# Products along the columns: read u in rows of eight, write the bank with a stride

## The chip, the cores and the metric

The kernel runs on one core of a Trainium2 chip. The core has a matrix engine (TensorE, PE in the profile, with its weight loads as PEld), a vector engine (VectorE, DVE), a scalar engine (ScalarE, ACT), GpSimd (POOL), and SyncE (SP), which issues the transfers here. Matmul results go to PSUM, which this kernel uses as eight banks of 512 fp32 values on each of 128 partitions; everything else on the chip lies in SBUF. The metric is the device time of one execution in microseconds. Before the change the median of three runs is 6957.4 us (6956.57 to 6957.86).

## The reference

Four layers are applied one after the other to an image batch x of shape (4, 192, 56, 56), all in fp32. The first three (a window attention with a convolution, a channel gate, an overlapping window attention with a gated feed-forward part) aren't touched. The last one is a selective scan in four directions, cut here to what matters:

```python
xn = _ln_cf(x, ln_w, ln_b)                                  # norm over the channels
xc, z = split(einsum('dc,bchw->bdhw', in_proj_w, xn))
xc = silu(depthwise_conv3x3(xc) + conv_b)                   # called u in the kernel
x_hw = xc.reshape(Bsz, D, L)                                # pixels by rows
x_wh = xc.transpose(0, 1, 3, 2).reshape(Bsz, D, L)          # pixels by columns
xs = stack([x_hw, x_wh, x_hw[..., ::-1], x_wh[..., ::-1]], axis=1)
x_dbl = einsum('kcd,bkdl->bkcl', x_proj_w, xs)              # 20 numbers a pixel and direction
dts, Bv, Cv = split(x_dbl, [R, R + N], axis=2)              # R = 12, N = 4
dt = softplus(einsum('kdr,bkrl->bkdl', dt_proj_w, dts) + dt_proj_b)
ys = _selective_scan(xs, dt, -exp(A_log), Bv, Cv) + Ds * xs # h = exp(dt A) h + dt B u ; y = C h
y = sum of the four directions, each put back in pixel order
out = x + einsum('cd,bdhw->bchw', out_proj_w, _ln_cf(y) * silu(z))
```

So x_proj (40 outputs for a pair of opposite directions, 192 inputs) is applied to u once in the order of rows and once in the order of columns.

## The kernel before

A layer is one function; the last is `layer3`. The 192 channels lie as two halves of 96 on the partitions (padded with zeros to 128), the 3136 pixels of an image along the free dimension. An image is cut into 7 chunks of 448 pixels: eight rows of 56, or, for the column directions, eight columns of 56.

For each of the four images b and each chunk c, `begin(b, c)` loads x, normalizes it (`layer_norm`, lines 1768 to 1789), projects it (line 1821), convolves with nine matmuls by diagonal matrices for each half (line 1851), applies SiLU and leaves u in one of two SBUF tiles `us[b % 2]`, pixels by rows. It ends with `product(b, 0, ...)` (called on line 1878): x_proj for the two row directions. `begin_columns(b, c)` waits until all seven chunks of an image are there, takes the eight columns of its chunk as a view of u and calls `product(b, 1, ...)` on line 1884.

`product` makes two matmul calls, one for each half of the channels, that accumulate into one bank (line 1893); an fp32 matmul call is two recorded instructions, so a product is four. ACT copies the 40 x 448 result to one of two `prod` tiles (line 1896), and SP writes it to a DRAM buffer `prods[b][o]` (line 1899), whose pixels are in the order of rows (o = 0) or of columns (o = 1).

A step of the scan is a chunk in one direction. `load` fetches the 12 rows for dt (line 1964) and, spread over partitions, B and C (line 1970); `sizes` makes dt (matmul 1985, softplus 1997); `decay` spreads dt over four states by transfers (line 2023) and exponentiates (2031); `scan` forms dt u on DVE (line 2046 by rows, 2049 with a column view of u), spreads it with PE (2056), multiplies by B (2062), scans on DVE (2078), multiplies by C on POOL (2085), sums over states with PE (2101) and adds to y (2106, 2111 or 2115; the last reads the bank with a stride to put columns back). Directions run in the order rows, columns, columns backward, rows backward. `final(b, c)` normalizes y, multiplies by the gate (line 1920, POOL), projects (1929), adds x (1940) and writes out.

The order of the work is set before anything runs, by a planner in the program, the class `Order`. Every piece of work is a generator that yields, ahead of each step, the engine, a planned duration and the tiles that it takes:

```python
def on_pe(n, *takes, ready=None):
    return "PE", 0.0019 * n, takes, None, ready
...
best.append((t + self.HURRY * th[0], th[1], t, th))   # earliest planned start, plus 0.05 us a place
```

The planner starts the piece with the smallest planned start plus a small term for its place, moves the clock of its engine on by the planned duration, and goes on. The instructions of PE, ACT, DVE and POOL, and with them the transfers on SP, are issued in that order, and each engine works its queue off in order. `product` plans `passes * n` columns of PE time: 2 passes for rows and 4 for columns, where n is 448. A change of a planned duration can thus change the order of everything behind it. The places are set at the end of `layer3`:

```python
order.add(n * (b - 1) + 6 * c + 4, begin(b, c))
order.add(n * (b - 1) + 48 + c, begin_columns(b, c))
order.add(n * (b + 1) - 2 * c, final(b, c))
```

Of the kernel before, what the change touches and what calls it, by code (L numbers as in the profile page):

```python
# [19 lines left out]
B, C, H, W = 4, 192, 56, 56  # L20
HW = H * W
HALF = 96
CH = 448
# [191 lines left out]
def load_packs(nc, pool, packs, aps):  # L215
    tiles = {}
    for name, pack in packs.items():
        t = pool.tile([pack.p, pack.n], F32, name=f"w_{name}")
        nc.sync.dma_start(t, aps[name])
        for n in pack.at:  # L220
            tiles[name + "." + n] = pack.view(t, n)
    return tiles
# [18 lines left out]
class Order:  # L241
# [20 lines left out]
    def take(self, kind="bank"):  # L262
        slot = min((s for s in self.kinds[kind] if s[0] is not None), key=lambda s: s[0])
        slot[0] = None
        return slot[1]

    def done(self, tile):

        (slot,) = (s for slots in self.kinds.values() for s in slots if s[1] is tile)
        slot[0] = self.end + self.LATENCY  # L270
# [53 lines left out]
def on_pe(n, *takes, ready=None):  # L324

    return "PE", 0.0019 * n, takes, None, ready
# [10 lines left out]
def on_act(*n, takes=(), table=None, ready=None):  # L337
    return "ACT", sum(0.2 + 0.0009 * i for i in n), takes, table, ready
# [6 lines left out]
def on_sp(*takes):  # L345
    return "SP", 0.5, takes, None, None
# [1329 lines left out]
def layer3(tc, src, packs, aps, dst):  # L1676
# [7 lines left out]
    nc = tc.nc  # L1684
    with ExitStack() as ctx:
        const = ctx.enter_context(tc.tile_pool(name="c_const", bufs=1))
        dram = ctx.enter_context(tc.tile_pool(name="c_dram", bufs=1, space=DRAM))
        w = load_packs(nc, const, packs, aps)
        inT = w["c128.inT"]
        in_b = const.tile([HALF, 4], F32, name="in_b")  # L1690
        with tc.tile_pool(name="c_ps0", bufs=1, space=PSUM) as ps0:
            pb = ps0.tile([HALF, 4], F32, name="pb")
            for m in range(4):
                for k in range(2):
# [4 lines left out]
                        start=(k == 0),  # L1699
                        stop=(k == 1),  # L1700
# [26 lines left out]
        def keep(name, shape, n, rows=128, zero=True):  # L1727

            tiles = [per.tile([rows, *shape], F32, name=f"{name}{i}") for i in range(n)]
            if zero:  # L1730
                for t in tiles:
                    nc.gpsimd.memset(t[HALF:], 0.0)
            return tiles

        us = keep("u", [2, HW], 2)
# [24 lines left out]
        def gone(*what):  # L1760
            return what in passed
# [30 lines left out]
        def begin(b, c):  # L1792
# [83 lines left out]
            nc.sync.dma_start(pixels(zmem[b])[:, :, c * CH : (c + 1) * CH], zt)  # L1876
            done(zt)
            yield from product(b, 0, px, u[:, :, px], 2)
            passed.add(("rows", b, c))

        def begin_columns(b, c):
            yield lambda: all(gone("rows", b, i) for i in range(NCHUNK))
            uv = us[b % 2].rearrange("p h (y x) -> p h x y", x=W)[:, :, 8 * c : 8 * c + 8]
            yield from product(b, 1, slice(c * CH, (c + 1) * CH), uv, 4)
            passed.add(("columns", b, c))

        def product(b, o, px, u, passes):

            n = px.stop - px.start
            yield on_pe(passes * n, "bank")  # L1890
            pp = take()
            for k in range(2):
                nc.tensor.matmul(pp[:40, :n], w["c128.xpT"][:, k, o], u[:, k], start=(k == 0), stop=(k == 1))  # L1893
            yield on_act(n, takes=("prod",))
            t = take("prod")
            nc.scalar.copy(t[:, :n], pp[:40, :n])
            done(pp)
            yield on_sp()
            nc.sync.dma_start(prods[b][o][:, px], t[:, :n])
            done(t)  # L1900
# [224 lines left out]
        n = 8 * NSC  # L2125
        for b in range(B):
            for c in range(NCHUNK):
# [3 lines that stand above are left out]
# [42 lines left out]
```

## Time and profile before

| | |
|---|---|
| median of three runs | 6957.4 us |
| the profiled execution | 6951.71 us |
| its span, first to last instruction | 6949.9 us |
| mean granted TensorE clock | 0.931 |
| PE busy | 5890.7 us (85%) |
| DVE busy | 5908.5 us (85%) |
| ACT, POOL busy | 2640.6 us (38%), 1423.8 us (20%) |
| line 1893, all products | 224 instructions, 149.5 us of PE |
| rows of that line | 128x448, x192; 128x504, x16; 128x392, x16 |

Times of single instructions come from one profiled execution. A row of a timeline is the start in us, the length, engine, line, operation, output<-inputs and the number of instructions; in brackets stands the idle time of the engine before it, and what ended it. A row of a table of stages is the stretch in us, its length, and for each engine the time in which it was busy, then the share of its full clock that TensorE was granted, the mean share of time that the transfer engines were busy, and the GB/s they moved. Groups and sources are named by the line of the kernel.

### The profile page before, as it was taken

The page shows a single profiled execution, that of the slowest core. Times are in us where ns is not written, and L with a number is a line of the kernel's source. Part 1 is how long each engine was busy: PE and PEld are TensorE (multiplying, and loading weights), DVE is VectorE, ACT ScalarE, POOL GpSimd, SP SyncE. Part 2 cuts the span into 40 slices and gives each one's busy share as a digit, 9 for nine tenths or more (in the row PEclk, how much of TensorE's full clock was granted, in tenths as well). Part 3 has the DMA queues.
Part 4 walks back from the last instruction along what each step waited for, and adds up shares of the span by engine and source line. Part 5 has one row for each costly group of instructions (what it writes and reads, how often), then busy time and mean ns, then how long its engine had stood idle before and what let it go on. Part 6 is the DMA issues. An engine that isn't in the chain of part 4 may idle for free. (4 is left out here: it accounts for less than half of the span.)

```text
span 6949.9 us, 107660 instructions
## 1 busy us (share of the span) xinstructions
PE 5890.7 (85%) x43810; PEld 2685.0 (39%) x43810; DVE 5908.5 (85%) x7379; ACT 2640.6 (38%) x4083; POOL 1423.8 (20%) x1409
## 2 busy tenths in 40 slices
PE   4999979999999994968888787885799989899776
PEld 2445434444444441345444444442332222222211
DVE  2799999999999999648999898997348788887897
ACT  1111112221122211135555455543256656556543
POOL 0000000000000000032222222220125445445564
PEclk9999989999999997979999899987899999999998
DMA  3222112221222112110000000000145555555654
GB/s 94 56 52 64 34 35 53 58 65 35 52 64 61 35 45 73 45 52 16 19 19 14 19 17 17 19 14 8 34 104 130 142 143 129 152 133 136 166 151 108
DMA packets 252044, 462.69 MB, mean 67 GB/s; under 512 B 30388, under 2 KB 237964, under 8 KB 240412
## 3 DMA queue, kind: packets, MB, share of 16 engines
q1 hardware_dynamic: 251548, 455.80, 25.8%
q8 instruction: 345, 5.65, 0.3%
q14 instruction: 151, 1.24, 0.1%
HBM read 238.58 MB, written 62.96 MB: 43 GB/s over the span
## 5 line engine op out<-in xcount | busy, mean ns | idle before, releaser
L789 DVE TENSOR_TENSOR pr<-vdx,attn 112x1792 f32<-112x1792 f32 (+4 forms) x720 | 1185.6, 1648 | 19.0
L634 PE MATMUL a_bank<-qk_in,w_a 64*49 64x392 f32 x9408 | 1156.3, 496 | 0.0
L2085 POOL TENSOR_TENSOR da<-st,bc 128x448 f32<-128x448 f32 x672 | 859.0, 1283 | 862.9 <-DVE st L2078 618.9
L794 DVE TENSOR_TENSOR oa<-oa,pr 112x1792 f32<-112x1792 f32 (+1 forms) x423 | 764.8, 1808 | 0.0
L634 PE MATMUL a_bank<-qk_in,wd 64*49 64x392 f32 x4032 | 689.6, 493 | 0.0
L2078 DVE TENSOR_TENSOR_SCAN st<-da,st,c_bank 128x448 f32<-128x448 f32 x576 | 646.6, 1132 | 0.0
masks.py:197 POOL MEMSET b_ident<- 128x128 f32 x1 | 0.2, 205 | 2856.0 <-DVE sc L1042 2856.0
L634 PEld LDWEIGHTS a_bank<-qk_in,w_a 64*49 64x49 f32 x9408 | 431.6, 120 | 394.1 <-issue 389.2
L2062 DVE TENSOR_TENSOR c_bank<-c_bank,bc 128x448 f32<-128x448 f32 x672 | 382.5, 618 | 153.1 <-PE c_bank L2056 152.5
L315 ACT ACT_TABLE_LOAD x378 | 485.0, 1283 | 6.6
L2031 ACT ACTIVATE da<-da,a_neg 128x448 f32<-128x448 f32 x672 | 414.1, 658 | 122.5 <-DMA da<-dt 117.9
L1343 DVE SCALAR_TENSOR_TENSOR bg<-bzpad,w_b,bg 128x448 f32<-128x448 f32 (+2 forms) x672 | 423.1, 684 | 0.0
L2101 PE MATMUL c_bank<-da,w_c 128*32 128x448 f32 x1344 | 349.5, 570 | 66.3 <-POOL da L2085 61.4
L1851 PE MATMUL c_bank<-pad,diag 128*96 128x448 f32 (+2 forms) x1008 | 396.8, 543 | 2.4 <-ACT pad L1832 2.3
L794 DVE TENSOR_TENSOR ob<-ob,pr 112x1792 f32<-112x1792 f32 (+3 forms) x282 | 393.0, 1394 | 0.0
L2056 PE MATMUL c_bank<-du,w_c 32*128 32x448 f32 x1344 | 257.8, 624 | 121.6 <-DVE du L2046 80.4
L869 PE MATMUL a_bank<-xc,w_a 128*128 128x448 f32 x672 | 296.8, 571 | 66.0 <-DVE xc L854 66.0
L878 ACT ACTIVATE hm<-a_bank,w_a 128x448 f32<-128x448 f32 x168 | 106.4, 634 | 637.4 <-PE a_bank L869 618.3
L634 PEld LDWEIGHTS a_bank<-qk_in,wd 64*49 64x49 f32 x4032 | 247.4, 119 | 256.5 <-issue 254.6
L1432 PE MATMUL bank<-bxn,w_b 128*128 128x448 f32 (+2 forms) x672 | 288.1, 557 | 24.8 <-DVE bxn L1215 18.6
L884 PE MATMUL a_bank<-hm,w_a 128*96 128x448 f32 x672 | 290.6, 564 | 21.3 <-ACT hm L878 21.3
L655 PE MATMUL a_bank<-qk_sum,w_a 64*49 64x168 f32 (+1 forms) x5376 | 277.7, 337 | 27.1 <-DVE qk_sum L625 25.2
(305 smaller groups left out, 9825.2 us busy)
## 6 DMA issues: line engine op xcount, KB each, us to landing
da<-dt SPq DMA_DIRECT2D x672, 224.0 KB
vdx<-vmem SPq DMA_DIRECT2D x168, 476.0 KB
bc<-prod SPq DMA_DIRECT2D x224, 224.0 KB
row<-x SPq DMA_DIRECT2D x56, 336.0 KB
x<-x SPq DMA_DIRECT2D x4, 2352.0 KB
vmem<-vt SPq DMA_DIRECT2D x56, 168.0 KB
xc<-x SPq DMA_DIRECT2D x56, 168.0 KB
mid<-xc SPq DMA_DIRECT2D x56, 168.0 KB
```

The lines of the kernel that those rows point to most:

```text
L315: self.nc.scalar.preload_act_table_set(table)
L634: nc.tensor.matmul(py[a][outs[g], : 7 * W].rearrange("p (y x) -> p y x", x=W), wt[halves[a], dx], q[halves[a], r, i0 + m : i0 + m + 7, dx ...
L789: nc.vector.tensor_mul(pr, vv, wt)
L794: nc.vector.tensor_add(og, og, before)
L869: nc.tensor.matmul(ph[:, :CH], w["a128.c1T"][:, k, 128 * m : 128 * m + 128], xt[:, k], start=(k == 0), stop=(k == 1),)
L1343: nc.vector.scalar_tensor_tensor(dst, x, wt[:, t : t + 1], dst, ALU.mult, ALU.add)
L1851: nc.tensor.matmul(rows2(pc[:HALF, : n * W]), diag[:, h, t], pad[:, h, at + t // 3 : at + t // 3 + n, t % 3 : t % 3 + W], start=(t == 0), ...
L2031: nc.scalar.activation(da, da, AF.Exp, scale=a_neg[:, k, g : g + 1])
L2062: nc.vector.tensor_mul(tiles[j][:, :SCH], tiles[j][:, :SCH], b_)
L2078: nc.vector.tensor_tensor_scan(sts[j][:, r], da[:, r], tiles[j][:, :SCH][:, r], first, ALU.mult, ALU.add)
L2085: nc.gpsimd.tensor_mul(da, sts[j], c_)
L2101: nc.tensor.matmul(py[32 * j : 32 * j + 32, :SCH], w["c128.sum"], das[j], start=True, stop=True)
```

## The change

The view of u that a column product reads keeps the order of the rows: for each of the 56 rows, the eight neighbouring elements of the chunk's columns. The result of each pixel goes to the same place of the bank as before (columns one after the other), which is now 56 elements away from the result before it. The planned PE time of a column product goes from 4 to 2 passes. The matmul of the row products, the copy, the write to DRAM and all that reads it are as they were.

```diff
         def begin_columns(b, c):
             yield lambda: all(gone("rows", b, i) for i in range(NCHUNK))
-            uv = us[b % 2].rearrange("p h (y x) -> p h x y", x=W)[:, :, 8 * c : 8 * c + 8]
-            yield from product(b, 1, slice(c * CH, (c + 1) * CH), uv, 4)
+            uv = us[b % 2].rearrange("p h (y x) -> p h y x", x=W)[:, :, :, 8 * c : 8 * c + 8]
+            yield from product(b, 1, slice(c * CH, (c + 1) * CH), uv, 2)
             passed.add(("columns", b, c))
...
             yield on_pe(passes * n, "bank")
             pp = take()
+
+            out = pp[:40, :n].rearrange("p (x y) -> p y x", y=H) if o else pp[:40, :n]
             for k in range(2):
-                nc.tensor.matmul(pp[:40, :n], w["c128.xpT"][:, k, o], u[:, k], start=(k == 0), stop=(k == 1))
+                nc.tensor.matmul(out, w["c128.xpT"][:, k, o], u[:, k], start=(k == 0), stop=(k == 1))
```

## The prediction

> **What bounds the kernel now.** I read the table of stages first, then PE's order of work around the changed products, then the rows of the instructions that resemble the new one. The last layer starts its work near 4960 us and ends with the span. Stages around the column products (us, then busy time of PE, PEld, DVE, ACT, POOL, the granted TensorE clock, DMA share, GB/s):
>
> ```profile
> 5129.72:5152.90 23.18, 23.18 (x31) 3.71 (x28) 6.35 (x8) 6.13 (x12) 3.62 (x3) 1.00 0.26 72
> ...
> 5461.00:5466.00 5.00, 5.00 (x10) 0.89 (x10) 5.00 (x8) 4.80 (x7) 3.39 (x4) 0.50 0.47 142
> 5462.00:5517.00 55.00, 53.59 (x149) 11.07 (x146) 44.04 (x60) 32.74 (x51) 26.96 (x22) 0.95 0.59 153
> 5515.00:5935.00 420.00, 369.76 (x1224) 119.18 (x1220) 337.86 (x434) 251.54 (x358) 204.37 (x169) 0.95 0.55 137
> ...
> 6500.00:6700.00 200.00, 141.97 (x468) 33.93 (x469) 193.28 (x253) 104.72 (x154) 120.88 (x93) 0.94 0.62 161
> ```
>
> In the first row PE has no idle time while DVE works 6.35 of 23.18 us: this is the run of all seven column products of image 0. In the third row (column products of image 1) PE is busy 97%, DVE 80%; images 2 and 3 look the same (53.01 and 51.83 us of 55). In the fourth PE has 88%. Only in the last part, with no convolution left, is DVE the bound (97%). So PE time of a column product lies mostly on the path. The timeline says so too:
>
> ```profile
> 5129.72 23.26 PE L1893 MATMUL c_bank<-u,w_c 128*40 128x448 f32 x28
> 5152.91 0.95 PE L2101 MATMUL c_bank<-da,w_c 128*32 128x448 f32 x6
> ...
> 5153.98 0.68 DVE L2106 SCALAR_TENSOR_TENSOR y<-u,d_sum,c_bank 96x448 f32<-96x448 f32 x1 [17.81 <-PE c_bank L2101]
> ...
> 5472.76 3.47 PE L1893 MATMUL c_bank<-u,w_c 128*40 128x448 f32 x4
> 5476.16 1.03 PE L2056 MATMUL c_bank<-du,w_c 32*128 32x448 f32 x6
> ```
>
> DVE stood idle 17.81 us because PE reached the sums of line 2101 only after the 28 column instructions. One product is two calls and four recorded instructions. The chain that ended last gives a column product 3.40 us and a 448-wide row product, which reads u densely, 1.63 us. PE's clock isn't the reason for the double price: the neighbouring line 2101 keeps its 0.95 us, and the first row's clock is 1.00.
>
> **Part one, the read.** The column product reads u with 56 elements (224 bytes) between neighbours: 23.26 us by 28 is 0.83 us an instruction, against 1.63 by 4 = 0.41 for the dense row product. DVE shows the same toll on the same view of u:
>
> ```profile
> L2046 DVE TENSOR_TENSOR du<-dt,u x112: 589/595/2599, 5045.5 to 6905.9; 96x448 f32<-96x448 f32 x112
> ...
> L2049 DVE TENSOR_TENSOR du<-dt,u x112: 946/965/1127, 5224.8 to 6785.9; 96x448 f32<-96x448 f32 x112
> ...
> L2111 DVE TENSOR_TENSOR y<-y,c_bank x56: 585/607/618, 5473.0 to 6926.9; 96x448 f32<-96x448 f32 x56
> ...
> L2115 DVE TENSOR_TENSOR y<-y,c_bank x112: 581/612/622, 5239.0 to 6800.1; 96x448 f32<-96x448 f32 x112
> ```
>
> The three numbers are minimum, median and maximum in ns. Line 2049 (u by columns) takes 965 against 595 for line 2046 (u by rows). The new read has runs of eight elements (32 bytes). Nearest row: line 1581 feeds PE 8x8 windows out of a wider image, 233 ns, and line 1639 feeds it 64 dense elements, 221 ns; 12 ns on 64 elements makes 84 on 448. So the new read costs between 0.41 and 0.41 + 0.08 = 0.49 us an instruction. Those windows aren't aligned and the runs of u are (they start at 224 y + 32 c bytes, all multiples of 32), so I take 0.41.
>
> **Part two, the write.** No matmul of this kernel writes neighbouring results apart, so this cost has to be bounded. Below: nothing. It can't be a gain, since the dense write is the row product's. Above, by the nearest row: line 2115 reads the very same pattern (stride 56 within the bank, runs over eight) in 612 ns, line 2111 dense in 607. A visit to a far place in a bank therefore costs no more than 612/448 = 1.37 ns with all fixed time counted in. One visit per element makes at most 448 x 1.37 = 0.61 us an instruction; if accumulating needs two (fetch and put back), 1.22 us.
>
> The Trainium skill speaks against the change: "PSUM — Partial Sum Buffer", Specifications (TRN2), gives the bank lines of two fp32 values and says that an access pattern that isn't contiguous slows matmuls significantly. With half of each line used, the cost by that rule would double, 0.41 to 0.83 us, exactly what the strided read costs today, and the gain would be nothing. Rows 2111 and 2115 show no such loss, but for reads by another engine at 1.3 ns an element. PE delivers a dense fp32 element each 0.41 us/448 = 0.9 ns, not much faster. I take "no cost" as likeliest because the only row with this pattern in a bank is 5 ns off the dense one, and keep both ends (0.41 and 1.22 us).
>
> **Part three, the plan.** The price that the planner uses goes from 4 to 2 passes: 0.0019 x 4 x 448 = 3.40 us becomes 1.70, the old and the (hoped) new measured price. With it the order on all queues may change: PE; the copy (line 1896) on ACT and the write (1899) on SP behind each product; loads (1964, 1970) and spreads (2023) on SP; products with C (2085) on POOL. Nothing is added or dropped: same four PE instructions, one copy, one transfer. I cost the reshuffle at nothing on average; it repeats image by image (the first column products start at 5468, 5943 and 6413), so what it hits it hits three times.
>
> **Part four, what covers what.** In image 0 SP issues the writes of the products one by one, 13.51 us for five, before the next spreads; they come sooner by as much as PE does. The copies alternate between two tiles, though. At 1.63 us a product a tile must be free again in 3.3 us; copy 0.53, issue 0.28, and a landing like the 3.88 us that the chain gives for a spread would make 4.7, so up to 0.7 us a product could be lost there. PE has other banks, so most of that is hidden: 0.8 us lost in all.
>
> **Sum.** Image 0: 23.19 - 7 x 1.63 = 11.8 us off PE with DVE waiting; less 0.8: 11. Images 1 to 3: 7 x (3.40 - 1.63) = 12.4 us off PE each, in a stretch where DVE has 44.0 us to do. Late next is DVE: at its densest share in this trace (193.28/200 = 0.966) the stretch can't fall below 45.6, so 9.4 is the most. And PE with gaps gets slow: in the second row, after 2.5 us of idleness, it ran at clock 0.50 for 5 us, a 504-wide row product there taking 3.58 us where others take 1.88. One more gap of this kind in an image eats a good part of its 2.5 us; I take 1.4 off: 8. Together 11 + 3 x 8 = 35 us. From this execution's own 6951.7 us that gives 6917; the median of the runs is 5.7 us above it, so 6922.
>
> **Rivals.**
> - *Hidden anyway.* The write is free, but after each stretch the scans, their products on POOL and the sums keep their latency, and DVE at 91% of 5515 to 5600 takes back most: 2 us an image are left. 11 + 6 = 17: 6940. For it: 11 us of DVE's idle time in the stretch is all there is. Against: the chain in that stretch is PE, piece after piece.
> - *The write costs what the read did.* 0.83 us an instruction, as the rule on bank lines has it: 6957. The plan then believes 1.70 and gets 3.4. For it: that rule[...]. Against: row 2115.
> - *Slower: fetch and put back.* Each strided result needs two visits to the bank: 1.22 us an instruction, 4.9 a product. Place: the seven products of each image. Image 0: 28 x (1.22 - 0.83) = +11; the others 84 x (1.22 - 0.85) = +31, of which some 70% is on the path: +22. 6957 + 33 = 6990; at 1.1 us, 6980. It decides from about 0.9 us an instruction on, sooner if the order built on the half price makes DVE wait for late results. For it: PE accumulates into the bank, DVE in row 2115 only reads.
> - *Doesn't do what it says*: runs of eight read no faster than single elements. Rows 1581 and 1639 exclude it (a double price would show as 50 ns and more, not 12).
>
> **Chances.** Free write and most of it passed on 0.44 (6908 to 6937); hidden 0.13; same price 0.17; slower 0.26. 0.2%, or 14 us, is about what a measurement here can tell from no change. Faster by more: 0.57 (a few of "hidden" fall short of it, a few of "same price" gain); within: 0.17; slower: 0.26. The range runs from 6905, a little better than DVE's bound allows in all three stretches, to 6985, within the slower case; about 0.05 lies below and 0.13 above.
>
> **What would show it.** Column instructions of line 1893 at 0.41 us back to back in a run of some 12 us near 5130 (read and write free); at 0.6, one visit; at 0.83, the rule; beyond 0.9, two visits. DVE's 17.81 us wait falls to about 6. In the stretches after 5450, DVE's share rises from 0.80 to above 0.9; if it doesn't, the gain was hidden. More rows with clock 0.50 would show the loss by gaps. Copies of line 1896 waiting for transfers would show the tiles. A gain above 50 us would mean that the new order, not the price, did it.

## The result, and the profile after

The changed kernel takes 6895.2 us (median of five runs, 6883.7 to 6905.7), before it 6957.9 us (five runs): a ratio of 0.991, interval 0.990 to 0.992, or 63 us less. The forecast was 6922 us, from 6905 to 6985: the right direction and about half of the gain, with the fast end of the range 10 us above the measured time. The profiled execution took 6895.2 us, with a span of 6893.4 us. From line 1893 on, the changed kernel's lines are two higher; the matmul is line 1895 there.

The stages that the prediction watched, after the change (columns as before):

```profile
5131.05:5141.69 10.64, 10.64 (x31) 3.19 (x28) 6.34 (x8) 5.33 (x11) 3.59 (x3) 1.00 0.55 144
5452.00:5507.00 55.00, 47.07 (x168) 13.54 (x166) 52.02 (x70) 33.55 (x53) 30.51 (x25) 0.93 0.63 169
5909.00:5964.00 55.00, 46.47 (x167) 13.77 (x165) 53.06 (x71) 34.87 (x55) 30.66 (x26) 0.96 0.63 169
6374.00:6429.00 55.00, 46.83 (x167) 13.81 (x165) 52.73 (x70) 35.16 (x55) 29.57 (x24) 0.96 0.63 167
```

The run of column products of image 0 is down from 23.2 to 10.6 us. In the 55 us from the first column product of images 1 to 3, DVE's share rose from 80 (82 at image 3) to some 95%, and PE's fell from 94% to 85% (the prediction's 97% was counted from the row product before): in the changed kernel the bound went over to DVE there. PE's timeline and DVE's wait behind it:

```profile
5131.05 10.72 PE L1895 MATMUL c_bank<-u,w_c 128*40 128x448 f32 x28
5141.70 0.95 PE L2103 MATMUL c_bank<-da,w_c 128*32 128x448 f32 x6
...
5142.83 0.68 DVE L2108 SCALAR_TENSOR_TENSOR y<-u,d_sum,c_bank 96x448 f32<-96x448 f32 x1 [5.34 <-PE c_bank L2103]
```

10.72 us by 28 is 0.38 us an instruction, where it was 0.83: read and write together cost nothing over a dense product, and DVE's wait fell from 17.8 to 5.3 us. PE's busy time over the whole kernel fell by 51 us, from 5890.7 to 5839.4. The time fell by more, 63 us in the medians and 56.5 us between the two profiled spans. So the price is unlikely to be the whole of it.

### The profile page after: what moved, and what is told of

The parts are those of the page before. It is cut to its first block, busy times and chain, and to the rows that moved or that the text cites. A ratio compares the mean times of both kernels' runs of the same rounds, so it can differ in the third digit from the quotient of the medians.

```text
span 6893.4 us, 107669 instructions
## 1 busy us (share of the span) xinstructions
PE 5839.4 (85%) x43810; PEld 2681.5 (39%) x43810; DVE 5904.1 (86%) x7379; ACT 2627.7 (38%) x4075; POOL 1431.6 (21%) x1409
## 5 line engine op out<-in xcount | busy, mean ns | idle before, releaser
L586 ACT ACTIVATE qk_in<-a_bank,qk_bias,qk_scale 64x224 f32<-64x224 f32 (+5 forms) x288 | 146.0, 525 | 410.7 <-PE a_bank L571 408.4
```

## The experiments

Two theories stood at first: P, that the shorter matmuls on a path bound by PE make the whole gain, and O, that they make what the prediction summed and the new order of the queues makes the rest. In all but the runs that are named as the changed kernel's, the new matmul is written so that the lines keep the numbers of before. Behind each time stands the ratio of its median to that of the kernel before on the same chip, with its interval; gains are counted against the same runs.

**Price and order apart.** The new matmuls with the old planned price:

```diff
-            yield from product(b, 1, slice(c * CH, (c + 1) * CH), uv, 2)
+            yield from product(b, 1, slice(c * CH, (c + 1) * CH), uv, 4)
```

> The new matmuls (read in eights, written with a stride) under the order of before: the planned price of a column product is left at 4 passes, so that every engine works its queue in exactly the order of before. If the shorter matmuls alone make the gain (theory P, price), the time is near that of the changed kernel, 6890 to 6910 us. If the price gives what the prediction summed and the new order gives the rest (theory O, order), it is near 6922 us, 6912 to 6932. Column instructions at 0.39 to 0.41 us in both. DVE's wait before the first sums of line 2106 behind the column products falls from 17.8 to about 6 us.

Measured: 6928.3 us, 0.995 (0.994 to 0.997), a gain of 32 us. The queues of this kernel hold the same instructions in the same order as those of before; only the column products are shorter. That is theory O's number, and close to the 35 us of the prediction's sum. DVE's wait behind the column products of image 0 falls here as in the changed kernel, but in the 55 us from the first column product of image 1 DVE is busy only 86% and PE 85% (images 2 and 3: 88% and 85%):

```profile
5147.35 0.68 DVE L2106 SCALAR_TENSOR_TENSOR y<-u,d_sum,c_bank 96x448 f32<-96x448 f32 x1 [5.27 <-PE c_bank L2101]
...
5457.00:5512.00 55.00, 46.73 (x161) 13.13 (x158) 47.40 (x65) 33.29 (x49) 30.27 (x25) 0.97 0.64 161
```

So the shorter products alone don't make DVE the bound there; the 95% came with the new order. The old matmuls with the new planned price, the other half alone (kernel before, `uv, 4` made `uv, 2`):

> The matmuls of before (read with a stride of 224 bytes, written densely) under the order of the changed kernel: only the planned price goes from 4 to 2 passes. Theory P: no gain from it, 6955 to 6975 us, since the order now counts on products that come 1.7 us later than planned. Theory O: 6930 to 6945 us, the some 28 us that the prediction's sum leaves over.

Measured: 6940.5 us, 0.997 (0.996 to 0.998), a gain of 20 us, with not one instruction made cheaper, and although the plan counts on products 1.7 us sooner than they come. Theory P falls. What is left of 63 us after the price's 32 is 31 us for the order.

**Other orders.** The new matmuls with 3 passes and with 1:

> The new matmuls, with a planned price of 3 passes, between the old and the new. Every order costs the same work, so what differs from the runs with 4 and 2 passes is the order alone. Theory P: 6890 to 6910 us like the others. Theory O: the order matters by some 20 to 30 us in no simple direction; 6890 to 6940.

> The new matmuls, with a planned price of 1 pass, half of what they take. Theory P: 6890 to 6910 us like the others. Theory O: anywhere from 6890 to 6940 us, apart from the run with 2 passes by 10 us or more.

Measured: 6918.9 us (0.994; 0.992 to 0.995) and 6904.4 us (0.992; 0.990 to 0.993). The work is the same in all four; with 4, 3, 2 and 1 planned passes the time is 6928, 6919, 6895 and 6904 us. The order is worth up to 33 us. The right price gave the lowest median, but 1 pass isn't told apart from it: the gains are 63 and 56 us and their intervals overlap, where theory O expected 10 us between the two.

**Which image's order.** Planned price 2 passes for one group of images only (the edit is shown against the run with the old order):

```diff
-            yield from product(b, 1, slice(c * CH, (c + 1) * CH), uv, 4)
+            yield from product(b, 1, slice(c * CH, (c + 1) * CH), uv, 2 if b == 3 else 4)
```

and likewise `4 if b == 3 else 2`, and `2 if b == 0 else 4`.

> The new matmuls; planned price 2 passes for image 3 alone, 4 for the others, so the order is that of before until the last image's column products (some 6390 us). Theory L (local: each image's new order pays in the stretch after its own products, where the final steps of the image before, or in the last image its own, meet the scans): the tail's 10 us and no more, 6918 us, 6912 to 6922. Theory C (chance: any other price shuffles the order, and the gain falls where it falls): no reason for the same 10 us, 6910 to 6940.

> The new matmuls; planned price 2 passes for images 0 to 2, 4 for image 3. Theory L: the changed kernel without the tail's 10 us, 6905 us, 6900 to 6912. Theory C: the order of the last image differs from both others, 6885 to 6925.

> The new matmuls; planned price 2 passes for image 0 alone. Theory L: some 5 us under the run with the order of before, 6920 to 6928. Theory C: the 12 us by which PE's planned clock moves at image 0 shift all that is planned behind it, so that the run may gain as much as the changed kernel, 6895, or lose, 6935.

Measured: 6911.6 us (6909.7 to 6913.8; ratio 0.993, 0.992 to 0.995), 6916.0 us (6911.3 to 6926.4; 0.994, 0.993 to 0.996) and 6927.4 us (6922.3 to 6929.7; 0.995, 0.994 to 0.997). As gains over before these are 46, 42 and 31 us, against 32 with the old order: 15 us come from the order of image 3, 10 from that of images 0 to 2, nothing to be seen from image 0 alone. The parts add up to 25 of 31 us. Theory L expected 10, 23 and about 5: the first two runs lie outside its ranges (the first by 0.4 us) and inside the wide ones of theory C, the third lies inside L's. The sizes aren't settled to better than some microseconds, since the intervals of these ratios reach 10 us to either side.

The traces place it more sharply. The n-th scan of line 2078, counted from 0, in the runs with the old order and with the order of image 3 (start in us, worked out from the two timelines; the last column is the difference):

```
scan   old order   order of image 3
   0     5074.8     -0.7
 336     6039.0     -0.5
 462     6391.9     -0.6
 504     6506.6     +0.7
 576     6662.6     -3.0
 642     6800.6     -2.3
 654     6843.9    -11.9
 666     6883.5    -16.4
```

Up to the column products of image 3 the two stay 0.5 to 0.7 us apart. Then some 2 us are won where the final steps of image 2 meet the first scans of image 3, nothing for 66 scans without final steps, and 14 us where image 3's own final steps meet its last scans. The stages of those 24 scans, old order first:

```profile
6800.55:6883.46 82.91, 57.48 (x176) 17.83 (x174) 66.99 (x83) 38.35 (x58) 36.85 (x29) 0.84 0.47 122
```

```profile
6798.25:6867.02 68.77, 53.27 (x176) 16.27 (x174) 63.24 (x83) 38.18 (x58) 37.77 (x29) 0.95 0.56 147
```

The same instructions take 83 us or 69. PE is idle for 25.4 us in the first and 15.5 in the second, and its granted clock is 0.84 against 0.95, with 4 us more for the same work. The stretch repeats: these 24 scans take 83.0 us in the kernel before and 82.8 to 83.0 us in all three runs of new matmuls that keep image 3's old order (4 passes throughout, 2 for image 0, 2 for images 0 to 2), but 68.8 us with image 3's order, 70.8 in the changed kernel and 68.6 with the old matmuls in the new order. So these 12 to 14 us hang on image 3's order and not on the matmuls.

An example of what PE waited for in the old order, in rows of POOL, of DVE, and of PE with the clock of its first six:

```profile
6835.63 2.07 POOL L1920 TENSOR_TENSOR row<-row,gate 96x896 f32<-96x896 f32 x1 [8.35 <-ACT row L1912]
6837.66 1.12 POOL L2085 TENSOR_TENSOR da<-st,bc 128x448 f32<-128x448 f32 x1
```

```profile
6836.68 2.59 DVE L2046 TENSOR_TENSOR du<-dt,u 96x448 f32<-96x448 f32 x1
```

```profile
6839.32 1.87 PE L2056 MATMUL c_bank<-du,w_c 32*128 32x448 f32 x6 [5.13 <-DVE du L2046]
6841.12 5.30 PE L1929 MATMUL c_bank<-row,w_c 128*96 128x448 f32 x8
...
6839.32:6841.10 1.78, 1.78 (x6) 0.51 (x6) 1.00 (x1) 1.77 (x4) 0.70 (x1) 0.50 0.42 153
```

DVE's product dt u takes 2.59 us instead of 0.60. It begins while GpSimd multiplies by the gate, and ends only 0.49 us after the product with C (line 2085) that GpSimd starts right behind that: it was held up by both, and so were the other products of 2.59 us in this trace's last final steps. PE stands 5.13 us behind it, some 2 us of them for the lengthening and the rest because DVE had other work first, and then runs slowly: 1.87 us for six that take 1.03, at a granted clock of 0.50, and 5.30 for eight that take 3.25. The Trainium skill ("SBUF — State Buffer", Who interferes with whom) says that a DVE instruction with two SBUF inputs contends with a GpSimd instruction that reads SBUF; these rows agree (2.59 us against 0.60). In scans 642 to 666 it happened three times in the old order, 2.59 us each, and twice in the order of image 3, with 2.33 and 1.52 us.

**Is it that collision?** Two ways to take it away. First, GpSimd multiplies only 8 of 448 columns (the gate isn't applied to the rest):

```diff
-            nc.gpsimd.tensor_mul(yn[:HALF], yn[:HALF], sz)
+            nc.gpsimd.tensor_mul(yn[:HALF, :, :8], yn[:HALF, :, :8], sz[:, :, :8])
```

> The new matmuls under the order of before; in each final step GpSimd multiplies 8 of the 448 columns by the gate and leaves the rest, so its output is not the reference's and only its time is read. All orders and waits stay. Theory K (collision): in the order of before, DVE's product dt u (line 2046) meets that 2.08 us multiply in the last image's final steps, takes 2.59 us instead of 0.60, and PE, which stands behind it for 5 to 6 us, goes slow; the new order meets it less. Then this run gains most of all, some 35 us: 6893 us, and the three short runs lie within 8 us of one another. Theory F (finals, but not this collision): the distances between the orders stay, and all three gain about the same, 15 to 25 us: 6905 to 6913 us here.

> The same shortened gate multiply (8 of 448 columns, output not the reference's) with the order that plans 2 passes for image 3 alone. Theory K: within 4 us of the short run with the order of before, since what told them apart, the collisions in the last image's final steps, is gone: 6889 us. Theory F: 15 us below it, 6890 to 6898 us.

> The same shortened gate multiply (8 of 448 columns, output not the reference's) in the changed kernel, so with its whole order. Theory K: within 8 us of the short run with the order of before, 6880 to 6893 us. Theory F: some 30 us below it, 6870 to 6882 us.

Measured: 6884.1 us (0.990; 0.988 to 0.991), 6871.2 us (0.988; 0.986 to 0.990) and 6863.6 us (0.986; 0.985 to 0.988). All gain, and all three are faster than either theory's ranges; the old order gains most (43 us, against 41 and 32), but the three don't come together: from the old to the new order it is still 20.5 us, where it was 31, and to that of image 3 still 13, where it was 15. Theory K, that they lie within 8 us, falls. By the medians the collision is a third of what the order gives, or less; their runs spread by 10 to 21 us, so the share is rough. In the traces of scans 642 to 666 it is about half: they take 74.0 us with the old order against 66.4 and 67.3 with the other two, so 7 to 8 us where it was 12 to 14. The short multiply also takes 2 us off each final step's own path, so even these shares aren't the collision's alone. Second, with all the work kept, the multiply in two halves, so that DVE can get in between:

```diff
-            nc.gpsimd.tensor_mul(yn[:HALF], yn[:HALF], sz)
+            for h in range(2):
+                nc.gpsimd.tensor_mul(yn[:HALF, h], yn[:HALF, h], sz[:, h])
```

> The new matmuls under the order of before, with the final step's gate multiply on GpSimd as two instructions of 448 elements instead of one of 896. Same orders, same work. Theory K (collision): DVE's dt u product can get in between the halves, so its longest falls from 2.59 to some 1.6 us, and the first half starts as soon as its own activation is done; 10 to 20 us are won here, 6908 to 6918 us. Theory F: the collision is a small part, less than 8 us won: 6920 to 6928 us.

> The changed kernel with the gate multiply in two halves, as a candidate that might beat it. Theory K: fewer collisions here, so less to win: 5 to 12 us, 6883 to 6890 us. Theory F: within 5 us of the changed kernel, 6890 to 6900 us.

Measured: 6920.0 us (6914.5 to 6922.2; 0.994, 0.993 to 0.996), a gain of 6 to 8 us over the old order, and 6894.7 us (0.991; 0.989 to 0.992), no gain over the changed kernel. The longest dt u of the last final steps fell from 2.59 only to 2.1 us: in the trace it waits for the second half and again for the product with C behind it. Those 24 scans still take 82.1 us. Again a part, of the size that theory F allows.

**A candidate.** The changed kernel with the gate multiply on DVE:

```diff
-            yield on_pool(2 * CH, each=0.0021)
-            nc.gpsimd.tensor_mul(yn[:HALF], yn[:HALF], sz)
+            yield on_dve(2 * CH)
+            nc.vector.tensor_mul(yn[:HALF], yn[:HALF], sz)
```

> The changed kernel with the gate multiply of the final step on DVE, planned there at its planned DVE price, so that it can't meet a DVE instruction. A candidate that might beat both. DVE gains 28 x about 1.07 us = 30 us of work and loses some 24 us of prolonged dt u products; each final step loses 1 us and a change of engine. Theory K: 6880 to 6895 us, at or below the changed kernel. Theory F, or a DVE that is the bound in the last part: 6900 to 6920 us.

Measured: 6903.0 us (0.992; 0.991 to 0.994), not better than the changed kernel. No dt u product by rows took over 0.8 us any more, so the collisions were gone: in the changed kernel they had made such products 23 us longer in all. But DVE has 28 instructions more, of 1.06 us, or 30 us. No version here beats the changed kernel.

**The disputed cost by itself.** A series of matmuls on zeros ahead of the last layer, one bank, groups of four accumulated, first fp32, then bf16 (the edit is shortened to its operands):

```diff
+ near = bt[:, :CH]; far = near.rearrange("p (x y) -> p y x", y=H)
+ by_row = bu.rearrange("p (y x) -> p y x", x=W)[:, :, 8:16]
+ by_col = bu.rearrange("p (y x) -> p x y", x=W)[:, 8:16]
+ far_c = near.rearrange("p (y x) -> p x y", x=8)
+ m(near, bw, bu[:, :CH]) ; m(near, bw, by_row) ; m(far, bw, by_row) ; m(near, bw, by_col) ; m(far_c, bw, by_col)
```

> The changed kernel with a series of matmuls on zeros ahead of the last layer's work (their results are used by nobody; the time of the whole is some 80 us longer and not compared). 128x40 weights, 448 columns, groups of four accumulated into one bank; fp32, then bf16, each: read and write dense; read rows of eight, write dense; read rows of eight, write with a stride of 224 bytes; read with a stride of 224 bytes, write dense; both with a stride. If a strided write costs nothing in any case: fp32 0.37 to 0.41 us a recorded instruction in the first three, 0.83 in the last two; bf16 the same pairs at its own price. If it is free only because fp32 delivers an element at half the rate of bf16 (the rule on lines of two values): bf16 with the strided write takes about twice its dense time. If the two tolls add up, the fifth takes more than the fourth.

Measured in one execution, in this order (line 1718 dense, 1720 read in eights, 1722 read in eights and written with a stride of 56 results, 1724 read with a stride, 1726 both with a stride, where results stand 8 apart):

```profile
4925.26 12.19 PE L1720 MATMUL trydt.float<-try_udt.float,try_wdt.float 128*40 128x448 f32 x32
4937.28 12.19 PE L1722 MATMUL trydt.float<-try_udt.float,try_wdt.float 128*40 128x448 f32 x32
4949.31 26.61 PE L1724 MATMUL trydt.float<-try_udt.float,try_wdt.float 128*40 128x448 f32 x32
4975.74 26.63 PE L1726 MATMUL trydt.float<-try_udt.float,try_wdt.float 128*40 128x448 f32 x32
5002.19 9.26 PE L1718 MATMUL trydt.bfloat<-try_udt.bfloat,try_wdt.bfloat 128*40 128x448 bf16 x48
5011.29 9.24 PE L1720 MATMUL trydt.bfloat<-try_udt.bfloat,try_wdt.bfloat 128*40 128x448 bf16 x48
5020.37 18.20 PE L1722 MATMUL trydt.bfloat<-try_udt.bfloat,try_wdt.bfloat 128*40 128x448 bf16 x48
5038.37 38.90 PE L1724 MATMUL trydt.bfloat<-try_udt.bfloat,try_wdt.bfloat 128*40 128x448 bf16 x48
```

An instruction, read in eights: fp32 0.381 us for both kinds of write, bf16 0.193 us dense and 0.379 us with the strided write. So a strided write of 448 results took some 0.38 us, 0.85 ns each, in both types: an fp32 instruction takes that long anyhow, while a bf16 one is doubled. Reads with a stride cost 0.83 us (fp32) and 0.81 us (bf16), some 1.8 ns an element whatever its type, and a strided write beside them adds nothing (26.61 and 26.63).

## Why the prediction was wrong

- *What bounds the kernel*: right that PE does. With the order held fixed, PE time taken off the column products came back nearly in full at image 0 and in part at images 1 to 3. DVE as the next bound there wasn't reached by the price alone (86 to 88%), only with the new order (95%).
- *The read in eights*: right, 0.38 us an instruction; the bound of 0.49 wasn't needed. The 12 ns behind it were a difference of means; the medians of lines 1581 and 1639 are both 216 ns. Whether alignment played a part no run shows.
- *The write*: right that it costs nothing, and right for the rows that it rested on. The rule of the skill, weighed against them there, shows in bf16 (a factor of 1.96) and not in fp32.
- *The sum of the prices*: right in its total, 35 us forecast and 32 measured (6928.3 us). By its terms: image 0 was put at 11 us, and the scans of the run with the old order stood 12.5 us nearer to those of before after it (from +5.9 to -6.6 us); the loss at the two tiles of the copies wasn't to be seen. Images 1 to 3 were put at 8 us each; around their column products the scans moved by about 6, 7.5 and 3, and gave back 3 us ahead of image 3's. So these terms were put too high. They come from one execution of each kernel, 21 us apart in span where the medians are 32 us apart, and are rough.
- *The step that failed* stands in part three, the plan: "I cost the reshuffle at nothing on average". The reshuffle was worth 31 us, as much as the price, and 20 us with the old matmuls. The prediction even said that what the order hits it hits image by image, but gave it no number and no range, so the range ended at 6905 on the fast side, 10 us above the measured time. Seven orders of the same work (1 to 4 passes, and three mixed) span 6895 to 6928 us; a range that took this in would have reached some 30 us lower. The last of the prediction's signs, a gain above 50 us, came true, but the order made half of the gain and not all of it. A hint of what an order can cost stood in its own row of line 2046 (589/595/2599), of which only the median was used: in the kernel before, 19 of these products took over 0.8 us, 28 us more in all than at their median.
- *What the order changed*, as far as shown: the time is won where final steps meet scans. In the changed kernel's trace, against that of the run with the old order, the scans gain 10 us around the final steps of image 0, 4 and 3 around those of images 1 and 2, and 12 in image 3's last scans. A part of it, a third or less by the medians and at most about half in image 3's last scans, is the collision of DVE's dt u products with GpSimd. The rest isn't settled. The trace of the short-gate run with the old order still has PE waiting, in 70 us of the last scans, 9.6 us for dt u and 9.0 us for the squares of the final steps' norms (line 1778); that these waits are the rest was not tried.
- *The rivals*: "hidden anyway", a gain of 17 us, is excluded by the run with the old order (32 us, by its interval 23 to 43); "same price" and the two visits to the bank by 0.38 us an instruction.

## What to carry to other kernels

A planned price is a part of a kernel like any instruction: where a planner sorts the queues, a change of a price has to be costed twice, once for the work and once for the order, and the order needs a range even when nothing speaks for a sign. Holding the price while changing the work, and the other way round, takes two runs and tells the two apart. And where a strided access must fall somewhere, look at what the other side of the instruction leaves room for: this fp32 matmul had no room on the read and all that was needed on the write.

## What the runs showed that was not expected

- The toll of a strided read is a time and not a share: 1.86 ns an element in fp32 and 1.81 ns in bf16. In bf16 that is 4.2 times the dense price, in fp32 2.2 times.
- PE with strided bf16 reads lost its clock though its queue never stood still: in the table of stages, with DVE, ACT and POOL at rest, the granted clock falls to 0.50 a few microseconds into the series, and the time of an instruction stayed at 0.81 us all the same, in line with a read that sets the pace. The fp32 series with the same read kept a clock of 1.00. Why the two differ is open.

```profile
5038.40:5044.00 5.60, 5.60 (x8) 0.87 (x7) 0.00 (x0) 0.00 (x0) 0.00 (x0) 0.79 0.00 0
5044.00:5050.00 6.00, 6.00 (x9) 1.06 (x8) 0.00 (x0) 0.00 (x0) 0.00 (x0) 0.50 0.00 0
5050.00:5076.00 26.00, 26.00 (x33) 4.25 (x32) 0.00 (x0) 0.00 (x0) 0.00 (x0) 0.50 0.00 0
```

- The changed kernel's runs spread by 22 us (6883.7 to 6905.7), those of before beside them by 4 (on other chips by 9 to 13). With the old order and the new matmuls the spread was 3 us, with the new order and the old matmuls 18. So it seems to go with the order; why is open.
